# Second attention of a two-layer kernel: rows of scores packed densely into PSUM banks for their transposes, and rows of five blocks scored in two equal parts

## The chip, the cores and the metric

The kernel runs on one core of one Trainium2 chip. The metric is the time of one execution on the device in microseconds (us); a kernel's figure is the median of several runs.

## The reference

Two layers run one after the other on x of 2048 tokens by 128 features, all in fp32. Each layer normalises x, computes a mixing s and a gate g of the normalised rows, and adds s * g to x.

```
x  = L0_attn_x[0]                      # 2048 x 128
# layer 0
xn = layernorm(x)
s  = relu attention of xn, 16 heads of 8
g  = silu(routed block of xn)          # 255 selected rows through attention and a feed-forward
x  = x + s * g
# layer 1
xn = layernorm(x)
q, k, v = xn @ W_Q + b_Q, xn @ W_K + b_K, xn @ W_V + b_V     # 16 heads of 64
w  = softmax(causal(q k^T / 8))                               # 16 x 2048 x 2048
s  = (w v) @ W_O + b_O
g  = silu(silu(xn @ gate) * (xn @ up) @ down)
x  = x + s * g
```

The change concerns the causal softmax attention of layer 1, which the code calls the second attention.

## The kernel before

The first 560 us or so are layer 0 and the feed-forward part of layer 1. The rest is the second attention. It works through eight pairs of heads; `pr` is the pair and `e` (0 or 1) the head of the pair. A **row** is a tuple (pr, c, h, e): the 128 queries of chunk c (0 to 15) of one head against the keys of half h (keys 0 to 1023 or 1024 to 2047). Because of the causal mask a row has `blocks_of(c, h) = min(8, c + 1 - 8 * h)` blocks of 128 keys. The softmax of each half has a maximum and a sum of its own; `ratios`, `shares`, `divided` and `output` join the halves later.

Rows are put into **slots**. A slot is what one score tile holds, 2 x 512 fp32 columns in PSUM, which is two banks. `four(c0, h)` makes the slots of two neighbouring chunks: where they have 1 and 2 blocks, one slot takes both chunks of both heads (four rows), where they have 3 and 4 blocks a slot takes one chunk of both heads (two rows), and from 5 blocks on a slot is one row. Two slots are a **turn**. The order of the slots is written out by hand in `order`; a pair of heads has 38 slots, so 19 turns. Written as the blocks of the rows of each slot, they are

```
T0   [5] [6]            T7   [8] [1,2,1,2]      T14  [8] [8]
T1   [5] [6]            T8   [8] [8]            T15  [5] [6]
T2   [1,2,1,2] [7]      T9   [8] [8]            T16  [5] [6]
T3   [8] [7]            T10  [3,3] [4,4]        T17  [7] [8]
T4   [8] [3,3]          T11  [8] [8]            T18  [7] [8]
T5   [4,4] [8]          T12  [8] [8]
T6   [8] [8]            T13  [8] [8]
```

`attention` is the loop over all 152 turns. The order of the instructions on TensorE (PE), VectorE (DVE) and ScalarE (ACT) is the order in which the program gives them; the waits between engines follow from the tiles. One iteration does this:

- `kept` copies finished sums z from PSUM (ACT, L1341).
- For both slots of the turn, `scores` runs the matmuls of q and k (PE, L1139) into a tile of tag s, of which there are two, so that a turn's slot takes the tile that the same slot of the turn before had. Queries and keys are kept as a high part and a low part in the fp32r type, stacked over 128 partitions; therefore each piece of up to 512 columns takes two matmuls (`part`). Then `maxima` adds the causal mask to the last block where the row touches the diagonal (DVE, L1156) and reduces the row to the negative of its maximum (DVE, L1157).
- The rows of the turn before, whose exponentials lie in SBUF (`p`), are transposed block by block. `packed` distributes their blocks over PSUM banks of four blocks, `turned` runs the transposes (PE, L1327) into tiles of tag t, of which there are three, and `evicted` copies each row's piece of a bank to SBUF (L1334). The copies of the first and second bank go to ACT, those of all others to DVE.
- `exponentials` of the new slots (ACT, L1167) with the sum of the row as a second result.
- A part of the products with v (`weigh`, PE, L1182) that earlier turns have made possible.
- `other` does up to two further steps that need a bank of tag t: projections of keys, queries or values for turns to come (L1049, L1099, L1084), `divided` (L1221) or `output` (L1234). The keys and queries are then split on ACT (L1070) and POOL (L1072, L1074), and the SP queue copies q (L1111).

In `packed`, the kernel before takes a row's blocks in pieces of four and a rest, and opens a new bank whenever a piece does not fit whole into what is left of the last one.

Of the kernel before, what the change touches and what calls it, by code (L numbers as in the profile page):

```python
# [16 lines left out]
AF = mybir.ActivationFunctionType  # L17
ALU = mybir.AluOpType
AX = mybir.AxisListType
# [3 lines left out]
P = 128  # L23
# [927 lines left out]
def layer1(ctx, tc, a, small, ident, x1, xn1T, row_load, out):  # L951
# [4 lines left out]
    l1 = SimpleNamespace()  # L956
    W, ffn_w = {}, {}
    K, V, Q, M, Z, ZS, WIDE = {}, {}, {}, {}, {}, {}, {}
# [158 lines left out]
    def blocks_of(c, h):  # L1117
        return min(8, c + 1 - 8 * h)

    def scores(rows):  # L1120


        t = l1.ps.tile([P, 2, 512], F32, tag="s", name="t")
        flat = t.rearrange("p a b -> p (a b)")
        where, at = [], [0, 0]
        for pr, c, h, e in rows:
            qc, c4 = c // 4, c % 4
            if (pr, qc) not in M:
                M[pr, qc] = l1.wk.tile([P, 2, 4, 2], F32, tag="tops", bufs=6, name="tops")
                Z[pr, qc] = l1.wk.tile([P, 2, 4, 2], F32, tag="sums", bufs=6, name="sums")  # L1130
            n = blocks_of(c, h) * P
            lo = 0 if len(rows) == 1 else 512 * e + at[e]
            at[e] += n
            where.append((lo, n))
            q, k = Q[pr, qc, e], K[pr, h, e]
            for x in range(0, n, 512):
                y = min(x + 512, n)
                for part in range(2):
                    nc.tensor.matmul(  # L1139
                        flat[:, lo + x : lo + y], q[:, part, c4 * P : (c4 + 1) * P], k[:, x:y],  # L1140
                        start=(part == 0), stop=(part == 1),
                    )

        def maxima():
            for (pr, c, h, e), (lo, n) in zip(rows, where):
                if len(rows) == 1:
                    es, x, mask = slice(e, e + 1), flat[:, :n], l1.mask_q
                    last = x[:, n - P :]
                elif e == 0:
                    es, x = slice(0, 2), t[:, :, lo : lo + n]  # L1150
                    last = x[:, :, n - P :]
                    mask = l1.mask_q.unsqueeze(1).to_broadcast([P, 2, P])
                else:
                    continue
                if h == c // 8:
                    nc.vector.tensor_tensor(last, last, mask, ALU.add)  # L1156
                nc.vector.tensor_reduce(  # L1157
                    M[pr, c // 4][:, h, c % 4, es], x, AX.X, ALU.max, negate=True
                )

        return maxima, (flat, where)

    def exponentials(rows, flat, where):
        p = l1.wr.tile([P, 1024], F32, tag="p", bufs=4, name="p")
        for row, (lo, n) in zip(rows, where):
            pr, c, h, e = row
            nc.scalar.activation(  # L1167
                p[:, lo : lo + n], flat[:, lo : lo + n], AF.Exp,
                bias=M[pr, c // 4][:, h, c % 4, e : e + 1],
                accum_out=Z[pr, c // 4][:, h, c % 4, e : e + 1],  # L1170
            )
            ex[row] = [p[:, x : x + P] for x in range(lo, lo + n, P)]
# [110 lines left out]
    left, last = {}, {}  # L1283
# [7 lines left out]
    pts, ex, todo, done, after = {}, {}, [], [], []  # L1291
    n_slots, due, r, waited = 0, 0, 0, 0

    def blocks(pr, c, h, e):

        key = (pr, c // 2, h)
        nb = blocks_of(c, h)
        few = blocks_of(c // 2 * 2 + 1, h) <= 4
        if (*key, e) not in pts:
            pts[(*key, e)] = l1.wr.tile(  # L1300
                [P, 4 if few else 8, 2, P], F32, tag="pt4" if few else "pt8", bufs=4, name="pt"
            )
        x = ex.pop((pr, c, h, e))
        return [(pts[(*key, e)], c % 2, x, lo, min(4, nb - lo)) for lo in range(0, nb, 4)]

    def packed(rows):

        banks, room = [], 0
        for row in rows:
            for x in blocks(*row):  # L1310
                if x[4] > room:
                    banks.append([])
                    room = 4
                banks[-1].append(x)
                room -= x[4]
        return banks

    def turned(banks, copies):
# [32 lines left out]
    def attention():  # L1351
# [8 lines left out]
        while r < len(turns) + 1 or todo or done or after:  # L1360
# [5 lines left out]
            for rows in slots:  # L1366
                maxima, what = scores(rows)
                maxima()
                new.append((rows, *what))
            evicted(turned(packed(old), [nc.scalar.copy, nc.scalar.copy, nc.vector.tensor_copy]))  # L1370
            for x in new:
                exponentials(*x)
# [96 lines left out]
```

## Time and profile before

| | us |
|---|---|
| median of 3 runs | 1535.13 |
| lowest and highest run | 1533.04, 1536.53 |
| the profiled execution, its own time | 1535.0 |
| its span, first to last instruction | 1532.2 |
| PE, matmuls busy | 1462.9 |
| DVE busy | 1109.7 |
| ACT busy | 961.6 |

The granted clock of TensorE is 0.989 over the span. The page of the profile has the busy time of each engine, the chain that ended last, and the costliest groups of instructions by line. Further views tell who waited for whom, the chain in order of time, and the instructions in order of time. PE stands for matmuls, PEld for the weight loads that go with them; the loads can run beside the matmul before. Ends of matmuls are modelled in the profile, so spacings are taken from the starts. A matmul of fp32 operands appears as two records, one of fp32r operands and a transpose as one.

### The profile page before, as it was taken

The page shows a single profiled execution, that of the slowest core. Times are in us where ns is not written, and L with a number is a line of the kernel's source. Part 1 is how long each engine was busy: PE and PEld are TensorE (multiplying, and loading weights), DVE is VectorE, ACT ScalarE, POOL GpSimd, SP SyncE. Part 2 cuts the span into 40 slices and gives each one's busy share as a digit, 9 for nine tenths or more (in the row PEclk, how much of TensorE's full clock was granted, in tenths as well). Part 3 has the DMA queues.
Part 4 walks back from the last instruction along what each step waited for, and adds up shares of the span by engine and source line. Part 5 has one row for each costly group of instructions (what it writes and reads, how often), then busy time and mean ns, then how long its engine had stood idle before and what let it go on. Part 6 is the DMA issues. An engine that isn't in the chain of part 4 may idle for free.

```text
span 1532.2 us, 27033 instructions
## 1 busy us (share of the span) xinstructions
PE 1462.9 (95%) x10374; PEld 886.6 (58%) x10374; DVE 1109.7 (72%) x1985; ACT 961.6 (63%) x2056; POOL 307.9 (20%) x409
## 2 busy tenths in 40 slices
PE   4999999999999968999999999999999999999997
PEld 2223333233222346777777777777777777777775
DVE  5798778877888646667667767767766767767775
ACT  2787778777888635556555655655655655655653
POOL 1000100024000001242242232232231242232210
PEclk9999999999999989999999999999999999999998
DMA  2000100000000210010001001001001001001000
GB/s 64 1 5 3 37 4 4 9 5 27 7 12 9 76 35 15 15 29 15 15 18 25 15 15 28 15 15 29 15 15 28 15 15 29 15 15 24 19 15 14
DMA packets 19681, 29.24 MB, mean 19 GB/s; under 512 B 5024, under 2 KB 13600, under 8 KB 19552
## 3 DMA queue, kind: packets, MB, share of 16 engines
q1 hardware_dynamic: 18864, 26.47, 7.4%
q8 instruction: 81, 1.33, 0.4%
q0 software_dynamic: 256, 0.79, 0.2%
q14 instruction: 48, 0.39, 0.1%
q10 hardware_dynamic: 432, 0.26, 0.1%
HBM read 7.69 MB, written 1.72 MB: 6 GB/s over the span
## 4 chain that ended last, share of the span: by engine, by line
PE 85%; DVE 7%; ACT 6%; issue 1%; DMA 0%; POOL 0%; ACTq 0%; DVEq 0%; POOLq 0%
PE t L1139 17%; PE z L1182 16%; PE t L1327 15%; PE t L801 13%; PE t L785 6%; PE m L1234 2%; PE m L1049 2%; PE m L1084 2%; PE t L695 2%; PE m L1221 2%; PE m L1099 2%; ACT rt L793 2%; ACT pt L1334 1%; DVE rt L795 1%; DVE junk L303 1%
## 5 line engine op out<-in xcount | busy, mean ns | idle before, releaser
L793 ACT ACTIVATE rt<-t 128x512 f32<-128x512 f32 x624 | 329.6, 608 | 73.4 <-PE t L785 72.5
L1157 DVE TENSOR_REDUCE tops<-t 128x1 f32<-128x1024 f32 (+4 forms) x320 | 334.7, 1063 | 53.4 <-PE t L1139 46.4
L1167 ACT ACTIVATE p<-t,tops 128x1024 f32<-128x1024 f32 (+7 forms) x384 | 330.6, 877 | 4.6 <-DVE tops L1157 4.6
L1139 PE MATMUL t<-k,q 128*128 128x512 f32 (+3 forms) x1280 | 319.0, 392 | 8.5 <-ACT p L1167 7.8
L1334 ACT COPY pt<-t 128x512 f32<-128x512 f32 (+2 forms) x320 | 149.2, 523 | 277.5 <-PE t L1327 277.5
L795 DVE TENSOR_SCALAR rt<-t 128x512 f32<-128x512 f32 x400 | 259.2, 684 | 36.7 <-PE t L785 31.9
L1327 PE MATMUL t<-ident,p 128*128 128x128 f32 x2176 | 278.0, 276 | 5.0
L801 PE MATMUL t<-rt,va 128*9 128x512 f32 x2048 | 268.2, 596 | 3.7 <-ACT part L817 3.7
L1182 PE MATMUL z<-pt,v 128*64 128x256 f32 (+1 forms) x2304 | 268.3, 374 | 0.5 <-ACT zs L1341 0.5
L1139 PEld LDWEIGHTS t<-k,q 128*128 128x128 f32 x1280 | 219.2, 189 | 81.3 <-issue 34.4
L1327 PEld LDWEIGHTS t<-ident,p 128*128 128x128 f32 x2176 | 244.4, 141 | 34.8 <-ACT pt L1334 17.2
L1182 PEld LDWEIGHTS z<-pt,v 128*64 128x64 f32 x2304 | 151.9, 136 | 87.3 <-issue 25.2
L1334 DVE COPY pt<-t 128x512 f32<-128x512 f32 (+2 forms) x320 | 180.5, 608 | 1.7 <-PE t L1327 1.7
L785 PEld LDWEIGHTS t<-qT,kT 32*128 32x128 f32 x1024 | 64.6, 181 | 185.2 <-ACT rt L793 112.1
L785 PE MATMUL t<-qT,kT 32*128 32x512 f32 x1024 | 156.9, 497 | 4.9 <-DVE rt L795 2.7
L1156 DVE TENSOR_TENSOR t<-t,mask_q 128x128 f32<-128x128 f32 (+1 forms) x192 | 65.1, 339 | 93.8 <-PE t L1139 85.0
L1072 POOL CAST q<-x 64x512 fp32r<-64x512 f32 x60 | 36.6, 610 | 409.1 <-ACT x L1070 407.3
L1167 ACT ACTIVATION_READ_ACCUMULATOR p<-t,tops 128x1 f32 x384 | 82.4, 215 | 0.0
L1224 DVE TENSOR_TENSOR zs<-zs,m 128x512 f32<-128x512 f32 x48 | 32.8, 688 | 67.1 <-PE m L1221 67.1
L1074 POOL TENSOR_TENSOR k<-x,k 64x512 fp32r<-64x512 f32 x60 | 76.2, 1271 | 4.6
L1074 POOL TENSOR_TENSOR q<-x,q 64x512 fp32r<-64x512 f32 x60 | 76.1, 1269 | 4.6
L1072 POOL CAST k<-x 64x512 fp32r<-64x512 f32 x60 | 36.5, 609 | 173.0 <-ACT x L1070 171.2
(244 smaller groups left out, 1097.1 us busy)
## 6 DMA issues: line engine op xcount, KB each, us to landing
q<-q SPq DMA_DIRECT2D x64, 256.0 KB
xin<-in_x SPq DMA_DIRECT2D x4, 256.0 KB
on<-part SPq DMA_DIRECT2D x64, 16.0 KB
wide<-inverse SPq DMA_DIRECT2D x32, 32.0 KB
out<-res SPq DMA_DIRECT2D x4, 256.0 KB
r_w<-in_w SPq DMA_DIRECT2D x2, 256.0 KB
mdram<-mrows SPq DMA_DIRECT2D x1, 512.0 KB
w_W_K<-in_W_K SPq DMA_DIRECT2D x1, 512.0 KB
```

Source lines behind the costliest of these rows:

```text
L785: nc.tensor.matmul(t, kT[rows, g, kb * P : (kb + 1) * P], qTs[qc, g][rows, :], start=True, stop=True,)
L793: nc.scalar.activation(rt, t, AF.Relu, scale=scale)
L795: nc.vector.tensor_scalar(rt, t, scale, 0.0, ALU.mult, ALU.max)
L801: nc.tensor.matmul(acc[32 * j : 32 * j + HD0 + 1, :], va[:, kb, 4 * g + j, :], r[j], start=(kb == 0), stop=(kb == NC - 1),)
L1072: nc.gpsimd.tensor_copy(high, x[half(e), :])
L1074: nc.gpsimd.tensor_tensor(low, x[half(e), :], high, ALU.subtract)
L1139: nc.tensor.matmul(flat[:, lo + x : lo + y], q[:, part, c4 * P : (c4 + 1) * P], k[:, x:y], start=(part == 0), stop=(part == 1),)
L1157: nc.vector.tensor_reduce(M[pr, c // 4][:, h, c % 4, es], x, AX.X, ALU.max, negate=True)
L1167: nc.scalar.activation(p[:, lo : lo + n], flat[:, lo : lo + n], AF.Exp, bias=M[pr, c // 4][:, h, c % 4, e : e + 1], accum_out=Z[pr, c // 4 ...
L1182: nc.tensor.matmul(l1.z[half(e), slot, lo:2, :], V[pr, h][:, kb, half(e)], pts[e][:, kb, lo:2, :], start=(kb == 0), stop=(kb >= n0 - 1), s ...
L1327: nc.tensor.transpose(t[:, k + b, :], x[lo + b], ident)
L1334: copy(dst, t)
```

## The change

`scores` cuts a row of exactly five blocks (640 columns) into two parts of 320 columns, one at the start of each bank of the score tile, where it was cut into 512 and 128 columns that lay one behind the other. The maxima, the mask and the exponentials of such a row read the tile through a view of two segments; the exponentials are still written to 640 columns in one piece.

`packed` compares, for the rows of a turn, the number of blocks divided by four and rounded up with the sum of the same number for each row alone. Where the first is smaller, the blocks are packed densely: a piece is cut so that it fills the bank that is open, before a new one is begun. Elsewhere it works as before.

```diff
@@ scores
-            where.append((lo, n))
+            step = n // 2 if n == 5 * P else 512
+            if n == 5 * P:
+                view = t[:, :, :step]
+            else:
+                view = flat[:, lo : lo + n]
+            where.append((lo, n, view))
             q, k = Q[pr, qc, e], K[pr, h, e]
-            for x in range(0, n, 512):
-                y = min(x + 512, n)
+            for x in range(0, n, step):
+                y = min(x + step, n)
+                at_x = lo + x // step * 512
                 for part in range(2):
                     nc.tensor.matmul(
-                        flat[:, lo + x : lo + y], q[:, part, c4 * P : (c4 + 1) * P], k[:, x:y],
+                        flat[:, at_x : at_x + y - x], q[:, part, c4 * P : (c4 + 1) * P], k[:, x:y],
                         start=(part == 0), stop=(part == 1),
                     )
@@ maxima
-            for (pr, c, h, e), (lo, n) in zip(rows, where):
+            for (pr, c, h, e), (lo, n, x) in zip(rows, where):
+                axes = AX.X
                 if len(rows) == 1:
-                    es, x, mask = slice(e, e + 1), flat[:, :n], l1.mask_q
-                    last = x[:, n - P :]
+                    es, mask = slice(e, e + 1), l1.mask_q
+                    last = flat[:, n - P : n]
+                    if n == 5 * P:
+                        last, axes = x[:, 1, n // 2 - P :], AX.XY
...
-                    M[pr, c // 4][:, h, c % 4, es], x, AX.X, ALU.max, negate=True
+                    M[pr, c // 4][:, h, c % 4, es], x, axes, ALU.max, negate=True
@@ exponentials
-        for row, (lo, n) in zip(rows, where):
+        for row, (lo, n, x) in zip(rows, where):
             pr, c, h, e = row
+            dst = p[:, lo : lo + n]
+            if n == 5 * P:
+                dst = dst.rearrange("p (a b) -> p a b", a=2)
             nc.scalar.activation(
-                p[:, lo : lo + n], flat[:, lo : lo + n], AF.Exp,
+                dst, x, AF.Exp,
@@ blocks
-        x = ex.pop((pr, c, h, e))
-        return [(pts[(*key, e)], c % 2, x, lo, min(4, nb - lo)) for lo in range(0, nb, 4)]
+        return pts[(*key, e)], c % 2, ex.pop((pr, c, h, e)), nb
@@ packed
+        rows = [blocks(*row) for row in rows]
+        n = [row[3] for row in rows]
+        dense = -(-sum(n) // 4) < sum(-(-x // 4) for x in n)
         banks, room = [], 0
-        for row in rows:
-            for x in blocks(*row):
-                if x[4] > room:
+        for pt, ci, x, nb in rows:
+            lo = 0
+            while lo < nb:
+                k = min(4, nb - lo)
+                if not room or (k > room and not dense):
                     banks.append([])
                     room = 4
-                banks[-1].append(x)
-                room -= x[4]
+                k = min(k, room)
+                banks[-1].append((pt, ci, x, lo, k))
+                room -= k
+                lo += k
         return banks
```

More of the change, by code (lines that the diff above doesn't have):

```diff
@@ L1157, in maxima, with exponentials @@
                 nc.vector.tensor_reduce(
-                    M[pr, c // 4][:, h, c % 4, es], x, AX.X, ALU.max, negate=True
+                    M[pr, c // 4][:, h, c % 4, es], x, axes, ALU.max, negate=True
                 )
-        return maxima, (flat, where)
-    def exponentials(rows, flat, where):
+        return maxima, (where,)
+    def exponentials(rows, where):
         p = l1.wr.tile([P, 1024], F32, tag="p", bufs=4, name="p")
-        for row, (lo, n) in zip(rows, where):
+        for row, (lo, n, x) in zip(rows, where):
             pr, c, h, e = row
+            dst = p[:, lo : lo + n]
+            if n == 5 * P:
+                dst = dst.rearrange("p (a b) -> p a b", a=2)
             nc.scalar.activation(
-                p[:, lo : lo + n], flat[:, lo : lo + n], AF.Exp,
+                dst, x, AF.Exp,
                 bias=M[pr, c // 4][:, h, c % 4, e : e + 1],
```

## The prediction

> **What bounds the kernel now.** I read the page's busy shares first, then the chain that ended last, then who waited for whom, and only then the order in time.
>
> ```profile
> PE 1462.9 (95%) x10374; PEld 886.6 (58%) x10374; DVE 1109.7 (72%) x1985; ACT 961.6 (63%) x2056; POOL 307.9 (20%) x409
> ...
> PE 85%; DVE 7%; ACT 6%; issue 1%; DMA 0%; POOL 0%; ACTq 0%; DVEq 0%; POOLq 0%
> ```
>
> TensorE is busy for 95% of the span and holds 85% of the chain; DMA and POOL hold none. In the second attention (from 578.6 us on) the turns repeat with a period of 117.5 us for each pair of heads, and the stretch 904.6 to 1022.1 us, one period, has PE busy for 116.4 us. So what PE stops spending there comes off the time, unless another engine's queue then holds PE up. The waits of PE's weight loads from 650 us on (engine, tile, line; who ended it; us in all, times, longest) name the two queues that do so:
>
> ```profile
> PEld t L1327 <- ACT pt L1334: 16.8, 58, 0.4
> PEld t L1139 <- ACT p L1167: 9.5, 28, 0.7
> ```
>
> The first is a transpose waiting for an eviction to free its PSUM bank, the second a score waiting for exponentials to free a score tile. The chain of waits shows the first (start, us, what), in a turn that transposes rows of 5 and 6 blocks:
>
> ```profile
> 909.80 1.58 PE t L1139 x8
> 911.38 0.45 PE t L1327 x4
> 911.83 0.02 issue
> 911.85 0.59 ACT pt L1334
> 912.45 0.04 issue
> 912.49 0.44 PE t L1327 x2
> 912.93 2.31 PE z L1182 x20
> ```
>
> The chain leaves PE after four transposes, runs through the copy of their bank, and returns for the last two. The banks hold 4, 1, 4 and 2 blocks; tag t has three, so the fourth reuses the first. The other five transposes cover only part of that copy. In time: the ninth transpose starts at 912.09, the tenth at 912.49 (usual spacing 0.109), the eleventh 0.16 later: 0.29 + 0.055 = 0.35 us lost. All eleven take 1.64 us up to the first z, where sixteen in a turn without this wait take 1.86; 1.86 - 5 x 0.109 = 1.31. The two answers are 0.35 and 0.33; I use 0.33.
>
> The weight loads of the 5-block row in the same turn (timeline, starts):
>
> ```profile
> 910.07 0.19 PEld L1139 LDWEIGHTS t<-k,q 128*128 128x128 f32 x1
> 910.30 0.19 PEld L1139 LDWEIGHTS t<-k,q 128*128 128x128 f32 x1
> 910.41 0.30 PEld L1139 LDWEIGHTS t<-k,q 128*128 128x128 f32 x2
> 910.75 0.19 PEld L1139 LDWEIGHTS t<-k,q 128*128 128x128 f32 x1
> ```
>
> Beside a matmul of 512 columns loads are 0.23 apart; through the two of 128 columns, 0.11 (the x2 line spans two, 0.11 apart). Columns stream at about 0.42 ns each (512 in 0.229, 384 in 0.171, 256 in 0.118 us), so 128 should take 0.06: the weight load is what 0.11 is.
>
> **What the Trainium skill says.** "TensorE: Matmul & The Clock Gate", LDWEIGHTS (loading the stationary operand), gives a load's time as columns / 1.2 ns, so 107 ns for 128 whatever the rows; the trace agrees (108 to 110 ns). "Perfetto Trace Analysis", Optimization Strategy, reads a gap that repeats on a saturated engine as a sign of too few buffers; the 0.37 us gap before the tenth transpose is that. "VectorE: DVE Perf Modes", Mode 1x (REGULAR), says the plain mode works for fp32, PSUM and odd strides alike, one result a cycle; the trace shows 640 elements reduced in 825 ns, but no two-segment reduction to one value.
>
> **The change part by part.** A period has 19 turns; I call them T0 to T18. Rows of T(n) are turned in the iteration that scores T(n+1).
>
> *Two equal parts.* T0, T1, T15, T16 have one row of 5 blocks each: 4 a period, 32 in all. Before: 512, 512, 128, 128 columns: 2 x 0.229 + 2 x 0.109 = 0.676 us. After: four of 320. Interpolated between 256 and 384, one takes 0.145 us, above the 0.109 of a load: 0.580. Gain 0.096, say 0.10; 32 x 0.10 = **3.2 us**. Ends: 0 (slower at crossing into the second bank) and 0.112 (pure streaming, 3.6). Mask, reduction and exponential keep their element counts (0.30, 0.825, 0.811 us); a segmented view I cost at nothing. Bounds: a gain has no reason; up to 0.1 us each, about the fixed part that two 320-element copies would pay twice, would hide behind the slack below except in T0, T1: 16 x 0.1 = 1.6 us at worst.
>
> *Dense banks.* The test compares ceil(blocks/4) with the rows' own bank counts summed. 5+6 = 11: 3 < 4, dense. T2 ([1,2,1,2] and 7): 13: 4 < 6, dense. T7 (8 and [1,2,1,2]): 4 < 6, but the banks come out as before. All others compare 4 with 4.
>
> 5+6: banks 4 / 1,3 / 3. No fourth bank, so no wait. Copies stay four, but ACT now has 4, 1, 3 (before 4, 1) and DVE 3 (before 4, 2). ACT gains a 3-block copy, 0.486 us, of which 0.38 counts, since successive ACT instructions overlap by about 0.1; DVE loses 0.681 + 0.415 - 0.548 = 0.55. ACT's copy stands ahead of the exponentials, and the next scores wait for those. The slack from the end of all exponentials to the next scores: scoring T16, 914.27 to 916.12, 1.85 us; T17, 921.78 to 922.65, 0.87; T1, 938.73 to 940.19, 1.46. Each holds 0.38 plus the 0.33 to 0.43 by which PE comes earlier. So three of four evictions (T15, T16, T0) give 0.33 each: 3 x 8 x 0.33 = **7.9 us**.
>
> The fourth, T1's, falls in the iteration that scores T2, and there the chain goes another way:
>
> ```profile
> 940.75 0.94 PE t L1139 x8
> ...
> 943.17 0.70 DVE tops L1157
> ...
> 943.96 1.29 ACT p L1167 x7
> ...
> 945.73 2.08 PE t L1139 x8
> 947.81 0.45 PE t L1327 x4
> ```
>
> Scores, maxima, exponentials, next scores: PE arrives 0.46 us early and waits. A shorter transpose stretch only lengthens that wait: gain 0. Does the extra copy delay it? ACT: copies at 942.96, + 0.48 (4 blocks) + 0.15 (1) + 0.38 (3) = 943.97 to 944.0; the exponentials started at 943.96, on DVE's word. So 0 to 0.05: **-0.2 us** over 8.
>
> T2: banks before 1,2,1 / 2 / 4 / 3, after 1,2,1 / 2,2 / 4 / 1. Still four: the fourth waits for the first's three copies, but eight transposes cover them instead of six: the gap shrinks by 0.22. I take 0.2 x 8 = **1.6 us**. The price is one more ACT copy of 2 blocks (0.39, 0.29 net) ahead of T3's exponentials; their first tile was free at 950.36, needed at 951.53: covered. If that cover went it would cost up to 0.3 x 8 = 2.4.
>
> The ring of three banks moves one place in four turns of a period. The next user of a DVE-evicted bank is then a transpose of the next iteration, some 4 us later, and the projections take ACT's banks: no new wait. POOL's splits and SP's copies of q move along, neither added nor passed.
>
> Sum: 3.2 + 7.9 + 1.6 - 0.2 = 12.5 us. From the profiled execution (1535.0, its span 1532.2) that is 1522.5; the median of three runs is 1535.13, 0.1 off. I say 1522.6.
>
> **Rivals.** (a) *Half of it:* slack that looks wide in one period is used up once PE comes earlier; T17's and T1's waits on exponentials take the bank gain, and T0, T1 lose the score gain to segmented views. Left: T15's bank 8 x 0.33 = 2.6, scores 1.6, T2 1.6: 5.8 us, 1529.3. For it: 28 such waits exist and T1's second score tile has only about 0.1 us to spare today; against: ACT is 63% busy. (b) *Slower:* ACT becomes the bound of the dense turns. Each puts 0.38 (32 turns) or 0.29 (8) ahead of the exponentials: if these gated the scores in all of them, 14.5 us more and every PE gain swallowed: 1549.6. It decides from a slack below about 0.4 us; T2's turn alone is below. (c) *The split isn't what it says:* 320 columns run at a slower rate. The projections' fp32 matmuls take 0.43 us a record of 512 columns, nearly twice the scores' 0.229; at that rate 320 columns take 0.27, a row 1.08, 0.40 more than before: 32 x 0.40 = 12.9, less the 9.3 of the banks: 1538.6. The 384- and 256-column forms speak against it.
>
> **How the numbers follow.** Likeliest 0.82, its own range 1519.5 to 1526; (a) 0.12; (b) and (c) together 0.06. The range 1518.5 to 1528 takes in the ends of the score gain and of T2, and part of (a). A measurement of this kernel can tell about 0.2%, 3 us. Faster by more 0.91, within 0.03, slower 0.06.
>
> **What would show it.** Scores of T0, T15, T16, T1 near 1.38 us a turn where they are 1.48; eleven transposes in 1.31 instead of 1.64; the transposes' wait for ACT copies down from 16.8 to some 4 us, left in the turns with 7- and 8-block rows (about 0.15 each) and T2; the scores' wait for exponentials up from 9.5 to 12 or so, longest 1.0 instead of 0.7, in T2's turn alone; a period of 116.0 instead of 117.5. Scores waiting in T16, T17 or T1 would mean (a) or (b).

## The result, and the profile after

| | before | changed |
|---|---|---|
| median, us | 1535.64 (4 runs) | 1523.69 (4 runs) |
| profiled execution, us | 1535.0 | 1523.8 |
| its span, us | 1532.2 | 1522.0 |
| one period of 19 turns, us | 117.53 | 115.95 |

The changed kernel takes 0.9923 of the time before (95% interval 0.9908 to 0.9938), 11.95 us less by the medians. The forecast was 1522.6 with 1518.5 to 1528.0 around it. The two profiled spans are less far apart, 10.2 us, and their mean granted clocks differ: 0.989 before, where most other executions of that kernel have 0.984, and 0.984 in the changed one. A period in the middle of the second attention runs at full clock in both and is the better measure. I read it between the first score matmuls of two turns T15, one pair of heads apart (from 904.64 us on before, from 903.40 on in the changed kernel).

The page of the changed kernel, busy shares and the chain that ended last:

```profile
PE 1454.0 (96%) x10374; PEld 887.2 (58%) x10374; DVE 1091.7 (72%) x1953; ACT 974.5 (64%) x2096; POOL 308.2 (20%) x409
...
PE 86%; DVE 6%; ACT 5%; issue 1%; DMA 1%; SPq 1%; POOL 0%; ACTq 0%; DVEq 0%; POOLq 0%
```

PE is still the bound. ACT has 40 instructions more (4 turns and T2, eight times), DVE 32 fewer. The waits of PE's weight loads in the changed kernel, from 650 us on (us in all, times, longest):

```profile
PEld t L1146 <- ACT p L1180: 11.0, 22, 1.3
PEld t L1347 <- ACT pt L1354: 3.7, 24, 0.2
```

The transposes' wait for evictions fell from 16.8 to 3.7 us, and no single one is over 0.2 us. The scores' wait for exponentials rose a little, and its longest from 0.7 to 1.3; that longest one is in the third pair of heads, in the others it is 1.1. The chain of waits of the changed kernel in T16's iteration no longer leaves PE:

```profile
908.46 1.48 PE t L1146 x8
909.94 1.20 PE t L1347 x11
911.14 2.31 PE z L1195 x20
```

Before, the chain had two pieces of these transposes, the first four and the last two, with an ACT copy between them. By starts all eleven now take 1.29 us up to the first z, where they took 1.64. The weight loads of the 5-block row in the same turn (timeline, start and length):

```profile
908.50 0.19 PEld L1146 LDWEIGHTS t<-k,q 128*128 128x128 f32 x1
908.64 0.19 PEld L1146 LDWEIGHTS t<-k,q 128*128 128x128 f32 x1
908.79 0.19 PEld L1146 LDWEIGHTS t<-k,q 128*128 128x128 f32 x1
908.94 0.19 PEld L1146 LDWEIGHTS t<-k,q 128*128 128x128 f32 x1
```

They are about 0.145 us apart, more than the 0.109 of a load: the stream of 320 columns sets the pace. In T2's iteration the chain still runs through the exponentials, as in the kernel before, but it comes to them through ACT's three copies, where it came through DVE's maxima:

```profile
938.13 1.72 PE t L1146 x12
939.85 0.45 PE t L1347 x4
940.30 0.02 issue
940.33 0.97 ACT pt L1354 x3
941.29 0.04 issue
941.34 1.29 ACT p L1180 x7
...
943.13 2.07 PE t L1146 x8
```

The eleven transposes of T1's rows take 1.29 us here too, 0.35 less than before, yet the iteration is no shorter: PE's matmuls stand idle for 0.8 us ahead of the next scores where it was 0.5.

Iteration by iteration (the turn that is scored; length from its first score to the next iteration's, changed less before, one period):

| scored | forecast | measured | what it is |
|---|---|---|---|
| T15 | -0.10 | -0.10 | score split |
| T16 | -0.43 | -0.45 | score split, banks of T15 |
| T17 | -0.33 | -0.34 | banks of T16 |
| T0 | -0.10 | -0.10 | score split |
| T1 | -0.43 | -0.39 | score split, banks of T0 |
| T2 | 0 to +0.05 | +0.03 | banks of T1, hidden |
| T3 | -0.20 | -0.22 | banks of T2 |
| period | -1.56 | -1.58 | |

No other turn of this period moved by more than 0.02. Eight such periods would make 12.6 us; the medians show 11.95, which their interval doesn't tell from 12.6. In the two traces the second attention is 11.0 us shorter, and two places account for most of the rest. The first pair of heads takes 0.8 us more up to its T15, where the other pairs gain 0.7: the clock is at half there for 6.8 and 3.4 us in the changed kernel's profile, for twice 3.4 us in the one before. And in the third pair T2's iteration is 0.28 us longer than before, not 0.03: ACT's first exponential starts 0.28 us later in the iteration than in the other pairs, and the profile puts its last wait down to DVE's mask of the turn's second slot (L1166).

```profile
825.40 0.37 ACT L1180 ACTIVATE p<-t,tops 128x128 f32<-128x128 f32 x1 [0.15 <-DVE t L1166]
```

The third pair shows this in four more of the kernels below (dense banks only, six blocks split too, and the two with the keys at turn 2); why it is this pair alone stays open.

### The profile page after: what moved, and what is told of

Its sections match the earlier page's. It is cut to its first block, busy times and chain, and to the rows that moved or that the text cites. A ratio compares the mean times of both kernels' runs of the same rounds, so it can differ in the third digit from the quotient of the medians.

```text
span 1522.0 us, 27063 instructions
## 1 busy us (share of the span) xinstructions
PE 1454.0 (96%) x10374; PEld 887.2 (58%) x10374; DVE 1091.7 (72%) x1953; ACT 974.5 (64%) x2096; POOL 308.2 (20%) x409
## 4 chain that ended last, share of the span: by engine, by line
PE 86%; DVE 6%; ACT 5%; issue 1%; DMA 1%; SPq 1%; POOL 0%; ACTq 0%; DVEq 0%; POOLq 0%
PE t L1146 18%; PE z L1195 16%; PE t L1347 16%; PE t L801 13%; PE t L785 7%; PE m L1247 2%; PE m L1049 2%; PE m L1084 2%; PE t L695 2%; PE m L1099 2%; PE m L1234 2%; ACT rt L793 2%; DVE rt L795 1%; DVE junk L303 1%; ACT p L1180 1%
## 5 line engine op out<-in xcount | busy, mean ns | idle before, releaser
L1354 ACT COPY pt<-t 128x512 f32<-128x512 f32 (+3 forms) x360 | 163.7, 518 | 269.6 <-PE t L1347 269.4
L1146 PE MATMUL t<-k,q 128*128 128x512 f32 (+4 forms) x1280 | 316.3, 390 | 11.9 <-ACT p L1180 11.2
L1347 PE MATMUL t<-ident,p 128*128 128x128 f32 x2176 | 271.0, 276 | 0.0
L1354 DVE COPY pt<-t 128x512 f32<-128x512 f32 (+3 forms) x288 | 163.3, 606 | 2.7 <-PE t L1347 2.7
L1166 DVE TENSOR_TENSOR t<-t,mask_q 128x128 f32<-128x128 f32 (+1 forms) x192 | 65.0, 338 | 98.7 <-PE t L1146 85.1
```

The source lines that it names most:

```text
L1146: nc.tensor.matmul(flat[:, at_x : at_x + y - x], q[:, part, c4 * P : (c4 + 1) * P], k[:, x:y], start=(part == 0), stop=(part == 1),)
L1347: nc.tensor.transpose(t[:, k + b, :], x[lo + b], ident)
L1354: copy(dst, t)
```

## The experiments

The theory: PE's order of work is the bound; a bank wait lasts as long as the copy of the bank that is reused exceeds the transposes between; a 128-column matmul is paced by its weight load; what is saved counts except in T2's iteration, where the scores wait for exponentials. The main rival: ACT, which gets more copies, gates the scores, so the wait only changes its name. Medians are in us, ratios are to the kernel before on the same chip; the period is that of the profile, the same one as above. The start of the second attention differs between profiled executions (578.6 to 581.5 us), with nothing changed ahead of it; that can move a single execution by up to 3 us and leaves periods alone.

| | median | ratio, 95% interval | period |
|---|---|---|---|
| dense banks only | 1527.84 | 0.9945, 0.9931 to 0.9958 | 116.24 |
| split only | 1533.28 | 0.9984, 0.9977 to 0.9991 | 117.18 |
| T2 as before | 1525.38 | 0.9931, 0.9918 to 0.9945 | 116.11 |
| small bank first | 1528.49 | 0.9948, 0.9935 to 0.9962 | 116.50 |
| third bank on ACT | 1527.55 | 0.9952, 0.9939 to 0.9966 | 116.33 |
| six blocks split too | 1523.82 | 0.9926, 0.9913 to 0.9940 | 115.97 |
| keys at turn 2 | 1515.30 | 0.9871, 0.9856 to 0.9886 | 115.08 |
| keys, and 7 blocks' rest first | 1514.92 | 0.9864, 0.9849 to 0.9879 | 114.90 |

The kernel before measured 1535.77 beside the first four and 1534.81 beside the last four.

**One part alone: the banks.** In the changed kernel, the cut and its views taken out:

```diff
-            step = n // 2 if n == 5 * P else 512
+            step = 512
...
-                    if n == 5 * P:
-                        last, axes = x[:, 1, n // 2 - P :], AX.XY
```

> The changed kernel with rows of five blocks scored in 512 and 128 columns again; only the dense banks stay. Theory (PE bound, the bank wait removed in three of four turns, T2's wait shortened, nothing from T1's rows): the period of 19 turns goes from 117.53 us before to 116.35 (three times 0.34, 0.22, less 0.04), so 8 x 1.18 = 9.4 us less than before, near 1526.2. Rival (the score split brings most, the banks only move the wait to the exponentials): 3 us less at most, 1532 to 1536.

The period is 116.24, 1.29 less than before: T16 -0.34, T17 -0.34, T1 -0.37, T2 +0.03, T3 -0.23. Each bank term is there at its forecast size. The median is 7.9 less than before, 1.6 short of the 9.4 that was expected, and eight periods give 10.3; the second attention began at 581.35 in this kernel's profile and at 578.58 before.

**The other part alone: the split.**

```diff
-        dense = -(-sum(n) // 4) < sum(-(-x // 4) for x in n)
+        dense = False
```

> The changed kernel with the banks packed as before; only the two equal parts stay. Theory (a weight load of 0.109 us sets the pace of the two 128-column matmuls, 0.10 us a row, four rows a period, all on PE's path): period 117.13 instead of 117.53, 3.2 us less than before, near 1532.4. Rival (the gain is hidden behind the waits for exponentials): no change, 1535.6. In the trace the eight score matmuls of T16 take 1.38 us and the eleven transposes keep their 1.64.

T15, T16 and T0 gain 0.10 each, T1 only 0.05, and the period 0.35 (2.8 us over eight; the medians show 2.5). T1's scores take 1.46 us where T16's take 1.38: the first weight load for T1's second tile waits for the exponentials of T0's second tile, 0.07 us. So of the 0.40 that the split could give in a period 0.05 is lost to that wait. In the changed kernel it is 0.08: there T1 gained 0.39 where the banks alone give 0.37. Transposes keep their 1.64.

**T2 back in its old banks.**

```diff
-        dense = -(-sum(n) // 4) < sum(-(-x // 4) for x in n)
+        dense = sorted(n) == [5, 6]
```

> The changed kernel with dense packing for rows of 5 and 6 blocks alone, so T2's rows go into banks of 1,2,1 / 2 / 4 / 3 again. Theory (eight transposes instead of six cover the copies of T2's first bank): period 116.17 instead of 115.95, 1.7 us more than the changed kernel. Rival (T2 has four banks either way and one copy more on ACT when dense, so dense packing costs or brings nothing there): same as the changed kernel or up to 2 us less.

T3's iteration loses 0.21 of its 0.22 us again, and the thirteen transposes take 1.88 us as before, where the changed kernel has 1.66. The chain of this kernel leaves PE in T3's iteration for the three copies of the first bank:

```profile
945.16 0.45 PE t L1347 x4
945.61 0.02 issue
945.63 0.37 ACT pt L1354 x2
946.00 0.05 issue
946.06 0.29 ACT pt L1354
946.35 0.04 issue
946.39 0.55 PE t L1347 x3
```

In the changed kernel it stays on PE:

```profile
945.20 1.56 PE t L1347 x13
```

The period is 0.16 longer than the changed kernel's, not 0.22; turns that this edit doesn't touch differ by up to 0.02 each and make the rest. The one extra copy on ACT had cost nothing that shows. So dense packing helped T2 although it saved no bank.

**Four banks, the small one first.** In the kernel before, only the order of a 5-block row's pieces is changed, which makes the banks 1 / 4 / 4 / 2:

```diff
-        return [(pts[(*key, e)], c % 2, x, lo, min(4, nb - lo)) for lo in range(0, nb, 4)]
+        at = [(4, 1), (0, 4)] if nb == 5 else [(lo, min(4, nb - lo)) for lo in range(0, nb, 4)]
+        return [(pts[(*key, e)], c % 2, x, lo, k) for lo, k in at]
```

> The kernel before with one edit: in packed, a row of five blocks gives its single last block first, so the banks of a 5 and 6 turn are 1 / 4 / 4 / 2, still four; the first is copied in 0.27 us and eight transposes stand between its last transpose and the fourth bank. Theory (what costs is a first bank whose copy is longer than the transposes that cover it, not the number of banks): the eleven transposes take 1.30 us as with three banks; three turns of a period gain 0.34, 8.1 us less than before, near 1527.5. Rival (a fourth bank in a turn costs in itself, by its handover): little change, 1533 to 1536.

The chain of waits of this kernel in T16's iteration:

```profile
911.72 1.58 PE t L1139 x8
913.29 1.20 PE t L1328 x11
914.49 1.66 PE z L1182 x13
```

The eleven transposes run through with four banks, in 1.29 us by starts, and T16, T17 and T1 gain 0.35, 0.34 and 0.36. It is the cover that counts: what stands between the last transpose of a bank and the first of its next use, against that bank's copies. A fourth bank costs nothing in itself. One more rival falls here: dense packing also takes a copy off DVE, and the gain might have come from that, but in this kernel ACT and DVE copy the same pieces as before (1 and 4 blocks, 4 and 2).

**The suspected cost doubled: the third bank on ACT too.**

```diff
-            evicted(turned(packed(old), [nc.scalar.copy, nc.scalar.copy, nc.vector.tensor_copy]))
+            banks = packed(old)
+            third = nc.scalar.copy if len(banks) == 3 else nc.vector.tensor_copy
+            evicted(turned(banks, [nc.scalar.copy, nc.scalar.copy, third]))
```

> The changed kernel with the third bank of the 5 and 6 turns copied by ACT too, so ACT has all four pieces and DVE none: 0.38 us more on ACT ahead of the exponentials in four iterations of a period. Theory (the scores after T16, T17 and T1 have slack for it, the scores after T2 have none): 0.38 us more in T2's iteration alone, period 116.33 instead of 115.95, 3.0 us more than the changed kernel. Rival (ACT gates the scores of all dense turns): 0.38 us in all four, 12 us more.

T2's iteration is 0.42 longer than before where the changed kernel has 0.03 more; T16, T17 and T1 stay within 0.01 of the changed kernel. The period is 0.38 longer than the changed kernel's, 3.0 us over eight; the medians are 3.9 apart. The chain of this kernel in T2's iteration shows the fourth copy where the exponentials began:

```profile
941.94 0.95 ACT pt L1354 x3
942.89 0.06 issue
942.95 0.51 ACT pt L1354
943.46 0.76 ACT p L1180 x4
...
945.13 2.07 PE t L1146 x8
```

So in three of the four turns ACT had room for even a second extra copy, and in T2's none. The rival that ACT gates all dense turns is out. The 0.39 us by which T2's iteration is longer than the changed kernel's is all of the added copy: with three copies ACT was already at its limit there.

**Rows of six in equal parts.** The condition `n == 5 * P` is widened to five or six blocks in slots of one row, with `step = n // 2`.

```diff
-            step = n // 2 if n == 5 * P else 512
+            step = n // 2 if n in (5 * P, 6 * P) and len(rows) == 1 else 512
```

> The changed kernel with rows of six blocks scored in 384 and 384 columns instead of 512 and 256. Theory (the split gains only where a matmul streams for less than the 0.109 us of a weight load; 256 columns stream for 0.118): four times 0.171 instead of 2 x 0.229 + 2 x 0.118, 0.01 us a row: no change, within 0.5 us of the changed kernel. Rival (equal parts gain in themselves, one bank each): 0.1 us a row as for five blocks, 3 us less.

The period is 115.97 against 115.95, and the median 1523.82 against 1523.69. Equal parts bring nothing in themselves; the 5-block split gains because it does away with matmuls that stream for less than a weight load. That it is the load, and not a fixed cost of a short matmul, shows in the kernel before: in T16 the two 128-column matmuls of the row start only 0.06 us apart (910.30 and 910.36), while the loads that run beside them start 0.11 apart, and the 512-column matmul behind them (910.46) is followed after 0.29 us instead of 0.23.

**Work put into T2's wait.** The projection of the third quarter of the keys is due one turn earlier:

```diff
-            (-1, values, 1), (1, queries, 2), (3, keys, 2), (5, values, 2), (7, queries, 3),
+            (-1, values, 1), (1, queries, 2), (2, keys, 2), (5, values, 2), (7, queries, 3),
```

> The changed kernel with the projection of keys that was due at the turn 3 of each pair put at turn 2, so PE does it in T2's iteration, where it waits some 1.1 us for exponentials. Theory (the iteration's length is set by scores, maxima and exponentials, and PE's wait there is what swallowed the fourth bank gain): T2's iteration grows by little (0 to 0.2 us), T3's and T4's together lose 0.8 to 1.0: 5 to 8 us less than the changed kernel, near 1517. Rival (PE was not idle there, or the keys' split on ACT delays what follows): no gain, or up to 3 us more.

PE in T2's iteration of this kernel (start, us, in order of time):

```profile
934.42 1.36 PE L1347 MATMUL t<-ident,p 128*128 128x128 f32 x11
935.71 1.30 PE L1195 MATMUL z<-pt,v 128*64 128x256 f32 x12
936.95 1.12 PE L1049 MATMUL m<-xn1T,w_W_K 128*128 128x512 f32 x2
937.87 2.07 PE L1146 MATMUL t<-k,q 128*128 128x512 f32 x8
```

The projection now stands where PE had waited. T2's iteration is 5.58 us long (5.57 in the changed kernel), T3's shrinks by 0.56 to 5.01 and T4's by 0.27: the period is 0.87 shorter, 7.0 us over eight. The median is 8.4 below the changed kernel's, a little more than the forecast's 8. In the trace the surplus lies in the first pair of heads, where this execution has half clock for 3.4 us alone. The period shows that PE's wait in T2's iteration was spare time. The fourth bank gain had gone into that wait, as the 1.29 us of T1's transposes in an iteration of the old length show.

**The cover rule in two more turns.** In addition, the 7-block row ahead of an 8-block row gives its rest of three first:

```diff
+            if j == 0 and n == [7, 8]:
+                banks += [[(pt, ci, x, 4, 3)], [(pt, ci, x, 0, 4)]]
+                continue
```

> The kernel with keys at turn 2, and in addition the rows of 7 blocks in T17 and T18 give their last three blocks first: banks 3 / 4 / 4 / 4 instead of 4 / 3 / 4 / 4, so eight transposes instead of seven cover a shorter first copy. Theory (the cover rule that the small first bank showed): fifteen transposes take 1.75 instead of 1.86 us in two turns of a period: 0.1 x 2 x 8 = 1.7 us less than with the keys alone. Rival (that 0.1 us is no bank wait): no change.

Both stretches of fifteen transposes fall from 1.86 to 1.73 us, and the iterations that score T18 and T0 by 0.14 each. T1's gives 0.08 back, because its scores now come earlier to the wait for T0's second tile (1.54 us instead of 1.47). Net 0.18 a period, 1.4 us over eight. The medians, 1514.92 and 1515.30, agree in sign, but their intervals overlap. By its period this is the fastest version that was run.

## Why the prediction was right

- **PE bound, savings count.** Right: six iterations became shorter, five by PE's own saving and T1's by all but 0.08 of it; T2's grew by 0.03, and the rest of the period stood still.
- **Two equal parts, 0.10 a row.** Right in three turns. The 0.145 for 320 columns was interpolated and measured as such. One figure of the working doesn't follow: 0.42 ns a column, where the first of the three matmuls beside it gives 0.45 (512 in 0.229 us). 128 columns would still stream in 0.06 us, so the conclusion holds. In T1 three quarters of the 0.10 are lost to the wait for T0's second score tile, which the prediction named under rival (a) and put at nothing in its sum; worth about 0.6 us in all.
- **Dense banks, 0.33 in three turns.** Right: 0.34 to 0.37 with the banks alone; of the prediction's two answers, 0.35 and 0.33, the transposes themselves gave the larger (1.64 to 1.29). The slack of 0.87 us and more that was read off for ACT held, and held for a second extra copy.
- **Nothing from T1's banks.** Right, and shown twice: extra work of ACT lengthens that iteration by its full size, extra work of PE by 0.01 to 0.02.
- **T2 gains by cover, not by a bank less.** Right: 0.22 against 0.20.
- **Segmented views cost nothing.** Right: reductions to one value over two segments of 320 take 824 ns (825 before), the exponentials 815 (811).
- **Which terms were off.** The period came out at 1.58 us where the sum had 1.56, and part of that closeness is luck: the bank terms were each a little larger than forecast, T1's split smaller. The sum also took all eight pairs as equal. In the profiles the first pair gains nothing up to its T15, under a halved clock whose length differs from execution to execution, and the third gains 0.26 less than the others. That the scores' longest wait would be 1.0 us was nearly right for most pairs (1.1) and too low for the third (1.3).
- **The rivals.** ACT as the bound (b) is excluded by the doubled cost, a slow 320-column matmul (c) by the spacing of its weight loads. Half of it (a) was real in T1's scores alone. That less work on DVE brought the gain, a rival that the prediction doesn't name, is excluded by the small bank put first.

What stays open: why the second attention begins up to 3 us later in some executions, and why T2's exponentials start later in the third pair. No run was made for either.

## What to carry to other kernels

Where a ring of PSUM banks wraps round inside a burst of transposes, compare the copies of the bank that comes up again with the transposes issued in between; ordering the pieces so that a small one stands first can do as much as a bank less. Cut matmuls so that none streams for less than its weight load takes, and expect nothing from cuts above that. Before a saving is counted, look which engine the next tile waits for in that iteration: where it is another, the saved time is a gap, and the gain comes back when work from a busier turn is put there.

## What the runs showed of the hardware

In these traces a weight load of 128 columns paces 128-column fp32r matmuls at 0.109 us, while 256 columns (0.118 us) are already paced by the stream: the line lies between the two.

Where an fp32 projection of 512 columns stands ahead of the scores, 0.6 us pass between the starts of the first two score matmuls, where it is 0.3 after most other work, so part of the projection's own time is counted in the stretch of the scores. That is why moving the projection shortened T4's scores as well (2.02 to 1.75 us); the forecast for that run counted T3 and T4 together, 0.8 to 1.0, and they gave 0.83.
